# Planes made without ScalarE-GpSimd round trips, outer products first, and three images in turn

## The chip, the core and the metric

The program runs on one NeuronCore of a Trainium2 chip. Five engines work side by side, each through its own list of instructions: TensorE (PE) multiplies, VectorE (DVE), ScalarE (ACT) and GpSimd (POOL) compute, and SyncE (SP) issues most of the transfers between memory and on-chip memory; ACT and POOL issue some too. Engines wait for one another by semaphores. The metric is the device time of one execution in microseconds (us), lower is better.

## What is computed

Two layers on four images of 96 channels and 128x128 points, each layer added to its input.

```python
x = x + _L0_conv_ref(_gn(x), ...)   # projection, depthwise conv, four scans along rows/columns, norm, output projection
x = x + _L1_conv_ref(_gn(x), ...)

# layer 1, per image
xr, x1, x2 = _relu_split_norm(x, sc1, sc2, res_coef, nc1, nc2)   # two halves, each normed over the image
key, qry   = conv3x3(x1, aw1), conv3x3(x2, aw2)                  # cut into 3x3 patches
w_attn     = softmax(key . qry / sqrt(C*9))                      # 96 x 96 x 3 x 3, one per image
o          = conv3x3(conv3x3(x1, aw3), w_attn)                   # the value map, filtered by w_attn
y2         = norm(conv3x3(x2, w_conv2)) * x1
out        = xr + conv1x1([norm(o), y2], w_full)
```

`norm(o)`, the norm of x2's convolution and the split's statistics each need a whole image before the next step begins.

## The kernel before

**Stages.** The first part projects all images (L620) and scans them (L841); it ends near 3294 us. For each image the rest is: `norm` (`ssm_output`: mean and root over channels, output projection, result `xnew`; then `split_norm`: one pass over `xnew` for statistics, a second that writes the halves x1 and x2), `attend` (convolutions, attention weights, filtering) and `close` (`attn_output`: final 1x1 convolution and sum).

**Image 0** is filtered with plain maps: `direct_maps` convolves padded maps x1d and x2d (L1956) and writes the value map `vd`. **Images 1 to 3** use a product form of the 3x3 convolution: every row is cut into tiles of four columns, and six linear combinations of a tile, its planes, are multiplied by six weight matrices; four sums of the six products give the outputs. `planes_of` makes planes from a row block, `store_planes` writes them to memory (x1p, x2p, vp), `attention` loads them back in strips of 12 rows (tiles `ya`, `yc`; `yb` is a copy by ACT, L1786) and `products` multiplies. Image 0 takes this form only for its last filter, so its value map is first lifted from `vd` to planes `vp` (`lift` in `attention`, 32 blocks of four rows).

**planes_of** takes three steps of a queue `later`, one per tick: `differences` (ACT L1328 scales, POOL L1329 subtracts), `inner` (ACT L1334 and L1335 scale what L1329 wrote; POOL L1336 to L1338) and `outer` (POOL L1343 to L1345, then the store). ACT and POOL so wait for each other within one set of planes. There are 96 sets from the halves (8 rows each), 66 from value maps (`vt`, half a strip each) and 32 from `lift`.

**products and outputs.** A call makes four products (planes 1, 3, 2, 4) into two PSUM pairs `a`, `b`, then the outer two (0, 5) into a third pair `c`; three pairs exist. ACT copies `a` (L1456), DVE combines it with `b` (L1441, L1442), writes two outputs (L1445), prepares the other two (L1448, L1449) and at last adds `c` (L1466).

**Order.** `co_run(left, right, pace)` interleaves two generators while the program is written: `left` yields the cost of what it just wrote, and `right` is advanced by pace times that. Beside image b's `attend` run, in this order, `close` of image b-1 and `norm` of image b+1 at pace 0.85 (1.5 beside image 0, where only the rest of image 1's `norm` runs). After the scan the framework's planner fixes each engine's list from this order and the data's dependencies. SBUF holds two images' planes at a time in memory (`planes[b % 2]`).

**Lines touched:** L1046 `split_norm` (halves' tiles, store by ACT's queue), L1313 `planes_of`, L1358 `products`, L1425 `outputs`, L1702 `pair_sets`, L1747 `attention`, L1914 `direct_maps`, L2065 `Image`, and the driver from L2155 on.

Of the kernel before, what the change touches and what calls it, by code (L numbers as in the profile page):

```python
# [17 lines left out]
C = 96  # L18
# [18 lines left out]
AR = 12  # L37
GROUP = 9
# [29 lines left out]
def kernel(  # L68
# [101 lines left out]
    def col(name, width=1):  # L170
        return small.tile([C, width], F32, name=name, tag=name)
# [874 lines left out]
    def split_norm(xnew, x1d, x2d, stats, keep, cnt, ps, side, planes):  # L1046


        with ExitStack() as pools:
# [93 lines left out]
            shift = col("shift", 2)  # L1143
            nc.vector.tensor_mul(shift, sa, navg)
            scale = col("scale", 2)
# [8 lines left out]
            up, low = col("up", 2), col("low", 2)  # L1154
# [9 lines left out]
            thr = col("thr")  # L1164
# [4 lines left out]
            def stored(i, m, h):  # L1169
                if planes:  # L1170
                    return planes_of(
                        later, p2, h, RS, lambda pl: store_planes(nc.scalar, m, i * RS, RS, pl)
                    )
                at = (i * RS + 1) * PW
                return lambda: nc.scalar.dma_start(m[:, at : at + RS * PW], h)

            for i in range(NS):
# [3 lines left out]
                for side_, m in ((0, x1d), (1, x2d)):  # L1181
                    n = RS * PP + 4 if planes else RS * PW
                    h = p2.tile([C, n], F32, name=f"half{side_}")
# [15 lines left out]
                for _ in range(6 if planes else 1):  # L1199
                    later.tick()  # L1200
                    yield 2.0 if planes else 3.5
# [111 lines left out]
    def planes_of(later, pool, t, r, then, most=RS):  # L1313
# [3 lines left out]
        def by_k(k, n=2):  # L1317
            return t[:, k : k + r * PP].rearrange("p (t k) -> p k t", k=TW)[:, 0:n]

        a2, n = AA * AA, r * PT  # L1320
        got = []

        def differences():
            df = pool.tile([C, TW, most * PT], F32, name="df", bufs=1)[:, :, :n]
            eo = pool.tile([C, 2, most * PT], F32, name="eo", bufs=1)[:, :, :n]
            pl = pool.tile([C, NP, most * PT], F32, name="pl")[:, :, :n]
            got.extend((df, eo, pl))
            nc.scalar.mul(eo, by_k(1), a2)  # L1328
            nc.gpsimd.tensor_sub(df, by_k(2, TW), by_k(0, TW))  # L1329
            later(inner)  # L1330

        def inner():
            df, eo, pl = got
            nc.scalar.mul(pl[:, 0:NP:5], df[:, 0:2], a2)  # L1334
            nc.scalar.mul(pl[:, 3], df[:, 1], AA)  # L1335
            nc.gpsimd.tensor_sub(eo, by_k(3), eo)  # L1336
            nc.gpsimd.tensor_add(pl[:, 1], eo[:, 1], eo[:, 0])  # L1337
            nc.gpsimd.tensor_sub(pl[:, 2], eo[:, 1], eo[:, 0])  # L1338
            later(outer)

        def outer():
            df, _, pl = got
            nc.gpsimd.tensor_sub(pl[:, 0:NP:5], df[:, 2:4], pl[:, 0:NP:5])  # L1343
# [932 lines left out]
```

## Time and profile before

| | |
|---|---|
| runs | 7006.94 us median of 3 (6998.66 to 7019.27) |
| profiled execution | 6989.58 us, its span 6987.6 us |
| busy over the span | PE 5408.1 us (77%), DVE 4667.8 (67%), ACT 3838.1 (55%), POOL 3828.8 (55%) |
| mean granted PE clock | 0.858 |
| rest of `direct_maps` beside image 1's `ssm_output` | 3294 to 3590 us |
| image 0's filter beside image 1's `split_norm` | 3590 to 4050 us |
| image 1 (close 0, norm 2) | 4050 to 5065 us |
| image 2 (close 1, norm 3) | 5065 to 6085 us |
| image 3 (close 2) | 6085 to 6870 us |
| close 3 | 6870 to 6988 us |

Busy time is a share of an engine's span; an engine that is idle because another holds its input shows that as idle time before an instruction, with the releaser named. In the tables that follow, a row by stage gives the length of a stretch and the busy time of each engine in it; a group row gives count, total and mean duration of equal instructions; a wait row names the waiting engine and line, then who released it, the total, the number of times and the longest.

### The profile page before, as it was taken

To read this page: it belongs to the slowest core of one execution; us is meant where nothing else is said; L and a number is where in the kernel's file an instruction comes from. 1 tells how busy PE (TensorE), PEld (TensorE's weight loads), DVE (VectorE), ACT (ScalarE), POOL (GpSimd) and SP (SyncE) were. 2 spreads that over 40 slices of the span, in tenths; PEclk is the share of its full clock that TensorE was granted. 3 is DMA by queue.
4 is the path that set the end of the run, shared out by engine and by line. 5 is a ranking of instruction groups with operands and counts; after the bars stand their busy time and mean duration, and the time that the engine had idled before them with its cause. 6 is when DMAs were issued, how large, how long until landed. Compare 5 with 4: busy or idle time off the path is not lost.

```text
span 6987.6 us, 74482 instructions
## 1 busy us (share of the span) xinstructions
PE 5408.1 (77%) x23256; PEld 2373.8 (34%) x23256; DVE 4667.8 (67%) x6155; ACT 3838.1 (55%) x4426; POOL 3828.8 (55%) x2988
## 2 busy tenths in 40 slices
PE   5889978878886549899953368976688976688877
PEld 2323323322221114443421134444244443345542
DVE  3257879979895579897343467565776565785457
ACT  1257767777875666675354444455544464543333
POOL 2236669879794449797249942338813348723110
PEclk9999989989896669999976679987889887899888
DMA  8766777856766666756765566554675554764346
GB/s 145 179 163 179 201 205 203 233 157 197 206 171 175 175 203 196 209 170 203 190 152 146 153 161 177 160 146 122 179 190 156 158 139 129 182 185 103 89 119 172
DMA packets 886278, 1183.98 MB, mean 169 GB/s; under 512 B 208190, under 2 KB 745350, under 8 KB 873404
## 3 DMA queue, kind: packets, MB, share of 16 engines
q1 hardware_dynamic: 805436, 1065.88, 57.8%
q10 hardware_dynamic: 64240, 74.93, 3.7%
q0 software_dynamic: 16208, 38.42, 2.0%
q8 instruction: 186, 3.05, 0.2%
q14 instruction: 208, 1.70, 0.1%
HBM read 771.50 MB, written 337.56 MB: 159 GB/s over the span
## 4 chain that ended last, share of the span: by engine, by line
PE 27%; POOL 18%; issue 17%; DVE 16%; DMA 11%; ACT 9%; SPq 2%; ACTq 0%; DVEq 0%; POOLq 0%
PE bank L620 11%; PE bank L1956 5%; DVE dA L841 5%; POOL df L1329 4%; PE two L1380 3%; POOL pl L1343 3%; DVE pBC L824 2%; POOL eo L1336 2%; PE pBC L734 2%; DVE dl L845 2%; ACT yb L1786 2%; POOL pl L1345 2%; POOL pl L1338 2%; POOL pl L1337 2%; POOL pl L1344 2%
## 5 line engine op out<-in xcount | busy, mean ns | idle before, releaser
L620 PE MATMUL bank<-y,wp 128*128 128x512 f32 (+3 forms) x3584 | 1316.3, 624 | 94.4 <-DVE z L496 37.8
L853 POOL TENSOR_TENSOR y<-y,dl 128x1024 f32<-128x1024 f32 x384 | 1052.3, 2740 | 267.4 <-DVE dl L845 234.6
L820 POOL TENSOR_TENSOR dl<-dl,u 128x1024 f32<-128x1024 f32 x384 | 1008.2, 2625 | 225.9 <-ACT dA L796 111.9
L841 DVE TENSOR_TENSOR_SCAN dA<-dA,pBC 128x512 f32<-128x512 f32 x768 | 981.6, 1278 | 30.7
L620 PEld LDWEIGHTS bank<-y,wp 128*128 128x128 f32 (+3 forms) x3584 | 458.7, 169 | 764.8 <-issue 655.5
L734 PE MATMUL pBC<-xr,wbc 60*128 60x512 bf16 (+1 forms) x1536 | 456.3, 402 | 332.7 <-DVE dA L841 260.3
L1380 PE MATMUL two<-ya,wd 128*64 128x192 f32 (+3 forms) x2376 | 606.9, 437 | 136.2 <-DVE ring L1466 54.0
L845 DVE TENSOR_TENSOR dl<-dA,pBC 128x512 f32<-128x512 f32 x768 | 528.6, 688 | 267.0 <-PE pBC L734 193.6
L1956 PE MATMUL bank<-y,wn 128*128 128x384 f32 (+5 forms) x2408 | 670.4, 503 | 28.5 <-DMA y<-x1d 10.7
L1786 ACT COPY yb<-ya 64x2376 f32<-64x2376 f32 (+1 forms) x220 | 467.9, 2127 | 267.3 <-DMA ya<-x2p 105.8
L663 ACT ACTIVATE dl<-pd,dtb 128x512 f32<-128x512 f32 x768 | 486.2, 684 | 185.1 <-PE pd L734 164.7
L1380 PE MATMUL two<-yb,wd 128*64 128x192 f32 (+3 forms) x2376 | 576.2, 418 | 9.9 <-ACT yb L1786 9.9
L1380 PE MATMUL two<-ya,wa 128*96 128x384 f32 (+1 forms) x528 | 263.6, 587 | 357.5 <-DMA ya<-vp 172.4
L824 DVE TENSOR_TENSOR pBC<-dl,pBC 128x512 f32<-128x512 f32 x768 | 527.5, 687 | 8.8 <-POOL dl L820 7.9
L1441 DVE TENSOR_TENSOR sd<-sd,two 128x384 f32<-128x384 f32 (+5 forms) x176 | 137.4, 780 | 554.6 <-ACT sd L1456 541.9
L1336 POOL TENSOR_TENSOR eo<-vt,eo 96x396 f32<-96x396 f32 (+1 forms) x66 | 89.2, 1352 | 656.6 <-ACT eo L1328 656.6
L796 ACT ACTIVATE dA<-dl,negA 128x1024 f32<-128x1024 f32 x384 | 420.3, 1141 | 2.3
L1956 PEld LDWEIGHTS bank<-y,wn 128*128 128x128 f32 (+3 forms) x2408 | 306.0, 167 | 324.0 <-issue 169.0
L1380 PEld LDWEIGHTS two<-ya,wd 128*64 128x64 f32 (+1 forms) x2376 | 276.5, 177 | 396.5 <-issue 181.4
L1195 DVE SCALAR_TENSOR_TENSOR half<-xn,thr,half 96x1024 f32<-96x1024 f32 x128 | 212.9, 1675 | 259.0 <-ACT half L1190 134.5
L734 PEld LDWEIGHTS <-wbc 60*128 60x128 bf16 (+1 forms) x1536 | 103.9, 96 | 770.5 <-issue 756.7
L663 ACT ACT_TABLE_LOAD x245 | 314.3, 1283 | 93.3 <-PE pd L734 86.1
(302 smaller groups left out, 10322.7 us busy)
## 6 DMA issues: line engine op xcount, KB each, us to landing
u<-zb SPq DMA_DIRECT2D x192, 1024.0 KB
yms<-y SPq DMA_DIRECT2D x96, 512.0 KB
y<-yms SPq DMA_DIRECT2D x64, 768.0 KB
xn<-xnew SPq DMA_DIRECT2D x128, 384.0 KB
ya<-vp SPq DMA_DIRECT2D x40, 1039.5 KB
y<-y SPq DMA_DIRECT2D x128, 258.2 KB
zb<-z SPq DMA_DIRECT2D x64, 512.0 KB
ya<-x1p SPq DMA_DIRECT2D x30, 1039.5 KB
```

The source lines that it names most:

```text
L620: nc.tensor.matmul(blocks(pz[p:e]), lhsT=ws[k][:, d, c : c + e - p], rhs=window(ys[k], at, d, n), start=(i == 0), stop=(i == len(terms) - 1),)
L663: nc.scalar.activation(dst, src, AF.Softplus, bias=bias)
L734: nc.tensor.matmul(p, lhsT=w[rows], rhs=xr[rows, at : at + CH], start=True, stop=True)
L796: nc.scalar.activation(live[m]["dA"], live[m]["dl"], AF.Exp, scale=negA[:, g % 3, k : k + 1])
L820: nc.gpsimd.tensor_mul(t, t, u_view(n))
L824: nc.vector.tensor_mul(p, live[n]["dl"][:, bass.ts(half, CH)], p)
L841: nc.vector.tensor_tensor_scan(h, h, p, init, ALU.mult, ALU.add)
L845: nc.vector.tensor_mul(live[n]["dl"][:, sl], live[n]["dA"][:, sl], live[n]["C", half])
L853: nc.gpsimd.tensor_add(v, v, t.rearrange("p (a b) -> p a b", b=W))
L1380: nc.tensor.matmul(of(to[p:e], r), lhsT=w[:, i, c : c + e - p], rhs=tiles(t[k][:, i], o, r), start=(k == 0), stop=False,)
L1786: nc.scalar.copy(yb[64 * h - 64 : 64 * h, :, :n], ya[0:64, :, h * PT : h * PT + n])
L1956: nc.tensor.matmul(pc[p:e, :n].rearrange("p (h w) -> p h w", w=W), lhsT=w[:, c : c + e - p], rhs=v[:, :, 0:W], start=(i == 0), stop=(i == ...
```

## The change

**Planes.** `planes_of` no longer scales intermediate results: ACT writes two scaled copies of the input (`x4`, `x2`) in one step, and POOL makes all differences and sums from them in the next (eight instructions on the same number of elements as the seven before). A second form, `at_once`, makes the same planes on VectorE alone with seven instructions; it serves all 32 lifted blocks and, of image 1's halves, all of x2 and every second block of x1 (24 sets). The remaining 138 sets stay with ACT and POOL. Stores of the halves move from ACT's queue to SP's.

**Products.** The outer two products are made first; ACT copies them out of PSUM (`ou`), and DVE writes all four outputs after the inner four.

**Order.** Lifting moves from beside image 0's filter into `direct_maps`, up to four blocks after each set of strips, the rest at its end. `split` is cut off from `norm`. Beside image b now run the split of image b+1, the close of image b-1 and the norm of image b+2, at pace 1.0; beside image 0 the rest of image 1's split and the norm of image 2. `xnew` is kept three times, and coefficients of the split in one tile `kept`, three times. Value tile and output tile become one (`own`).

```diff
-        def differences():
-            ...
-            nc.scalar.mul(eo, by_k(1), a2)
-            nc.gpsimd.tensor_sub(df, by_k(2, TW), by_k(0, TW))
-            later(inner)
-        def inner():
-            nc.scalar.mul(pl[:, 0:NP:5], df[:, 0:2], a2)
-            nc.scalar.mul(pl[:, 3], df[:, 1], AA)
-            nc.gpsimd.tensor_sub(eo, by_k(3), eo)
-            nc.gpsimd.tensor_add(pl[:, 1], eo[:, 1], eo[:, 0])
-            nc.gpsimd.tensor_sub(pl[:, 2], eo[:, 1], eo[:, 0])
-            later(outer)
-        def outer():
-            nc.gpsimd.tensor_sub(pl[:, 0:NP:5], df[:, 2:4], pl[:, 0:NP:5])
-            nc.gpsimd.tensor_sub(pl[:, 4], df[:, 2], pl[:, 3])
-            nc.gpsimd.tensor_add(pl[:, 3], df[:, 2], pl[:, 3])
-            then(pl)
+        def at_once():
+            df, eo, pl = tile("df", TW, 1), tile("eo", 2, 1), tile("pl", NP, bufs)
+            stt = nc.vector.scalar_tensor_tensor
+            nc.vector.tensor_sub(df, by_k(t, 2, TW), by_k(t, 0, TW))
+            stt(eo, by_k(t, 1), -a2, by_k(t, 3), ALU.mult, ALU.add)
+            nc.vector.tensor_add(pl[:, 1], eo[:, 1], eo[:, 0])
+            nc.vector.tensor_sub(pl[:, 2], eo[:, 1], eo[:, 0])
+            stt(pl[:, 0:NP:5], df[:, 0:2], -a2, df[:, 2:4], ALU.mult, ALU.add)
+            for i, f in ((3, AA), (4, -AA)):
+                stt(pl[:, i], df[:, 1], f, df[:, 2], ALU.mult, ALU.add)
+            later(lambda: then(pl))
+        def scaled():
+            x4 = pool.tile([C, most * PP], F32, name="x4", bufs=1)[:, : r * PP]
+            x2 = tile("x2", 2, 1)
+            nc.scalar.mul(x4, t[:, : r * PP], a2)
+            nc.scalar.mul(x2, by_k(t, 1, TW)[:, 0:TW:2], AA)
+            later(lambda: differences(x4, x2))
+        def differences(x4, x2):
+            f, pl = tile("df", TW, 1), tile("pl", NP, bufs)
+            nc.gpsimd.tensor_sub(f, by_k(t, 2, TW), by_k(x4, 0, TW))
+            nc.gpsimd.tensor_sub(x2[:, 0], x2[:, 1], x2[:, 0])
+            nc.gpsimd.tensor_sub(x2[:, 1], by_k(t, 4)[:, 0], by_k(t, 2)[:, 0])
+            nc.gpsimd.tensor_sub(pl[:, 0:NP:5], f[:, 2:4], f[:, 0:2])
+            for i, x in ((1, f[:, 1:3]), (3, x2)):
+                nc.gpsimd.tensor_add(pl[:, i], x[:, 1], x[:, 0])
+                nc.gpsimd.tensor_sub(pl[:, i + 1], x[:, 1], x[:, 0])
+            later(lambda: then(pl), 2)
+        return at_once if vector else scaled
...
     # split_norm: store of a half's planes
-                        later, p2, h, RS, lambda pl: store_planes(nc.scalar, m, i * RS, RS, pl)
+                        later, p2, h, RS, lambda pl: store_planes(nc.sync, m, i * RS, RS, pl),
+                        vector=vector(i, m is x2d),
...
-                    yield 2.0 if planes else 3.5
+                    yield 2.5 if planes else 3.5
...
     # products: the two outer products are made ahead of the four
+        outer, sums = evac
+        ...
+        outer(a)
         a, b = pairs_of(ps), pairs_of(ps)
         ...
-        finish(c)
...
     # outputs
+                nc.scalar.copy(got[1], c[:m, :, :n])
...
+                nc.vector.tensor_add(u, u, got[0][:, :, 0])
+                    for k, x, f, y in (
+                        (0, s[p:e, 1], 1.0, u[p:e, 0]),
+                        (1, d[p:e, 1], AA, d[p:e, 0]),
+                        (2, s[p:e, 1], AA * AA, s[p:e, 0]),
+                        (3, d[p:e, 1], AA * AA * AA, u[p:e, 1]),
+                    ):
...
     # direct_maps
+            def lift(rows):
+                for _ in range(4 if rows < H else H // LR):
+                    ...
+                    nc.sync.dma_start(to, src[:, :, 1:PW])
+                    later(planes_of(
+                        later, img.lifts, h, LR, lambda pl, a=a: store_planes(nc.sync, img.vp, a, LR, pl),
+                        LR, True,
+                    ), 2)
+                    yield 1.2
+            yield from pair_sets(img, taps, later, p2, 3, inputs, convolve, lift)
+            yield from lift(H)
...
     # driver
+    light = chain(
+        imgs[1].norm(yms[0][1], psr, "right"),
+        imgs[1].split(psr, "right", lambda i, second: second or i % 2 > 0),
+    )
...
+        if 0 < b and b + 1 < NB:
+            after.append(imgs[b + 1].split(psr, "right"))
         if b:
-            light.append(imgs[b - 1].close(psr, "right"))
-        if b + 1 == 1:
-            light.append(next_norm)
-        elif b + 1 < NB:
-            imgs[b + 1] = Image(b + 1)
-            light.append(imgs[b + 1].norm(yms[(b + 1) // 2][(b + 1) % 2], psr, "right"))
+            after.append(imgs[b - 1].close(psr, "right"))
+        if b + 2 < NB:
+            imgs[b + 2] = Image(b + 2)
+            after.append(imgs[b + 2].norm(yms[b // 2 + 1][b % 2], psr, "right"))
-        co_run(left, light, 0.85 if b else 1.5)
+        co_run(left, light, 1.0 if b else 1.5)
         drain(left)
         drain(light)
```

## The prediction

> **What bounds the kernel now.** I read the table by stage first, since the average over the span mixes a scan, convolutions and small tails. All instruction lists are equal up to the end of the scan (3294 us); only what follows counts. Columns: length, then busy us of PE, weight loads, DVE, ACT, POOL, then clock, DMA share, GB/s.
>
> ```profile
> 3294.00:3590.00 296.00, 268.64 (x1125) 121.01 (x1121) 108.92 (x222) 124.77 (x196) 59.93 (x65) 0.95 0.65 175
> 3590.00:4050.00 460.00, 142.86 (x408) 60.72 (x408) 177.67 (x195) 199.64 (x264) 417.16 (x629) 0.62 0.60 152
> 4860.00:5065.00 205.00, 132.80 (x405) 57.76 (x405) 151.00 (x147) 108.95 (x105) 171.43 (x176) 0.79 0.64 165
> 6310.00:6720.00 410.00, 336.67 (x2338) 225.56 (x2336) 203.48 (x320) 165.89 (x161) 94.06 (x112) 0.87 0.40 97
> 6720.00:6870.00 150.00, 117.68 (x412) 52.99 (x412) 89.03 (x129) 50.35 (x33) 0.00 (x0) 0.88 0.55 140
> ```
>
> Row 1 is PE bound (91%). In row 2 POOL is busy 91% and PE 31%: image 0's filter waits for planes. Rows 4 and 5 are image 3 with nothing beside it: PE is 82% busy in the strips. The statistics L1868 of its strips start 51.1 us apart (6311 to 6669); beside `ssm_output` of image 3, in image 2, they are 78.6 us apart (5291 to 5606, four strips), beside `close` 63 to 79.
>
> Next the waits, for 3590 to 4050 (first four) and 6360 to 6710 (last two):
>
> ```profile
> PE two L1380 <- DMA ya<-vp: 172.4, 8, 42.6
> ACT pl L1334 <- POOL df L1329: 117.1, 45, 8.1
> ACT eo L1328 <- POOL pl L1338: 56.9, 26, 5.3
> SPq L1352 <- POOL pl L1345: 209.7, 30, 15.2
> PE two L1645 <- ACT sd L1456: 41.7, 14, 4.8
> ACT pl L1334 <- POOL df L1329: 36.1, 14, 3.9
> ```
>
> PE waits for `vp`, which SP stores only when POOL has made it. Even alone, image 3's transposes wait 41.7 us in some seven strips for ACT's copy, and in the same stretch ACT stands 36.1 us behind a scaling that waits for POOL.
>
> The groups give the price of planes (3590 to 4050: first two; 4683 to 5036: third and fourth; 6310 to 6720: last):
>
> ```profile
> L1329 POOL TENSOR_TENSOR df<-half 96x1056 f32<-96x1056 f32 x30 | 66.6, 2219 | 22.0 <-DVE half L1195 20.7
> L1329 POOL TENSOR_TENSOR df<-lift 96x528 f32<-96x528 f32 x32 | 38.8, 1212 | 5.1 <-DMA lift<-vd 4.9
> L1448 DVE TENSOR_TENSOR sd<-sd 96x384 f32<-96x384 f32 x8 | 11.2, 1399 | 0.0
> L1195 DVE SCALAR_TENSOR_TENSOR half<-xn,thr,half 96x1024 f32<-96x1024 f32 x30 | 48.9, 1637 | 32.5 <-ACT half L1190 17.2 <-POOL eo L1336 15.1
> L1448 DVE TENSOR_TENSOR sd<-sd 128x384 f32<-128x384 f32 x14 | 8.4, 599 | 0.0
> ```
>
> [...] L1448 takes 599 ns where POOL is 23% busy and 1399 ns where it makes planes. [...]
>
> **The change part by part.**
>
> *Planes on POOL.* Summed over its seven rows a half's set takes 9.1 us, a lift's 5.0 us. The new eight have the same elements; I take the same. 24 halves and 32 lifts leave POOL: 24 x 9.1 + 32 x 5.0 = 378 us, nearly all from 3590 to 4050.
>
> *Planes on DVE.* No row shows them. [...] I take 3.05 and 5.0: 32 x 3.05 + 24 x 5.0 = 218 us.
>
> *ACT.* Per half before 1156 + 642 + 411 ns; after, two scalings of 1056 and 528 elements, about 1.17 + 1.16. Copying the outer products adds 0.79 or 0.48 us a call, 118 us over all images; the removed sets give 81, and fewer intermediate scalings some more. ACT is at most 45% busy, so this is free. What counts is the wait: it now depends on POOL only through single buffers `x4`, `x2`. This frees part of the 41.7 us above: 15 us per image for images 1 to 3, -45 (bounds 0 and -41.7 x 11/7 x 3 = -197).
>
> *Outputs.* DVE per 128-row call: before 2 x 0.954 + 2 x 0.912 + 0.599 + 0.567 + 1.553 = 6.45 us, after 2 x 0.954 + 0.957 + 4 x 0.912 = 6.51. Nothing in time, but elements with two SBUF inputs rise from 1536 to 2304. The outer pair comes free by an ACT copy while the four products run, so PE need not wait for it; covered by these, at worst 0.8 us a call.
>
> *Lifting in `direct_maps`.* In the built order 20 lifts stand before the softmax, 12 between it and the last product weight. The 20 cost DVE 61 us of 187 idle ones, but their loads and stores stand in SP's list ahead of loads `y<-x1d` of a PE-bound stretch: 0 to 60 us, I take 10. The 12, with three sets of a half, six halves and the weights themselves, are 37 + 16 + 9 + 4 = 66 us of DVE ahead of `watd`, which took 9 us from L1593 to its issue: +57. Without this cover the same work would lie in row 2.
>
> *Image 0's filter with image 1's split.* DVE has left: 20 sets x 5.0 + 26 halves x 1.3 + 11 strips x 8.4 (two at 0.95, one at 0.96, four at 0.88, three statistics at 0.68) = 226 us; at 87% filling 260. POOL has 8 sets, 73 us. So DVE replaces POOL as bound.
>
> *Norm of image 2.* The split uses up the pace; in the built order all of this norm's PE work follows the filter's last product, and SP's first `y<-yms` stands behind the split's last store. It runs alone. Its round is a chain (copy L960, transfer `mq<-st`, DVE, root, ACT, PE): copies L960 start 14.1 us apart beside `direct_maps`, 18.2 beside image 1, and 7.6 at the shortest. Alone I take 10: 16 x 10 + 20 = 180 us (142 to 246).
>
> So image 1 starts at 3590 + 10 + 57 + 260 + 180, and 10 for statistics and first loads: 4107. Before, its first product is at 4080. **+30**.
>
> *Image 1.* Same content as before (split, close, norm), other order: 0. The bounds: ACT freed earlier, -60; POOL and DVE exclude each other more beside strips, +60.
>
> *Image 2.* Loses a norm: 4 x (78.6 - 51.1) = **-110**. Image 3 keeps its content. Stores from ACT's to SP's list: 96 x 0.5 us of issuing leave ACT; on SP they wait for POOL with `ya` loads behind them, which are issued half a strip ahead (25 us) of their use; that hides a POOL up to that late. Beyond, PE waits for each.
>
> Sum: 30 + 0 - 110 - 45 = -125 by the middles. The unpriced risks (SP's order, exclusion) are one-sided, so I give back 25: **-100**. Span 6987.6 - 100 = 6888; the profiled execution would be 6890, and since the median lies 17 above the profiled run, 6905 us.
>
> **Rivals.**
> - *More is freed.* ACT no longer holds PE, 100 of the 197, and the norm's round takes 8: 6905 - 55 - 30 = 6820. For: min round 7.6. Against: `x2` is one buffer that POOL frees with its last two instructions.
> - *The lone norm eats it.* Round 14.1 as beside `direct_maps` (+66) and DVE sets at 5.6 (+15), SP costs 20: 7005, no change. For: the chain is mostly latency. Against: beside `direct_maps` it waits for a PE that is 97% busy (235.9 of 244).
> - *Slower: exclusion beside strips.* Split now goes beside 6.2 strips of 38.6 cost units (240 / 38.6) in images 1 and 2. Per strip POOL has 5.2 halves' sets and two `vt` sets: 5.2 x 9.1 + 2 x 7.1 = 62 us, DVE 8 us of new and 6 of old two-input work. If none overlaps, a strip takes 76 instead of about 65, and with ACT held by `x2` 82: 2 x 6.2 x 17 = +210: 7115. It decides against me when such strips pass 73 us. For: L1448's 1399. Against: POOL's 9.1 already has such waiting in it.
> - *The change doesn't do what it says:* ACT still waits as long for POOL. Then only -110 + 30 is left, inside the main range.
>
> **Numbers.** Main 0.50 (6845 to 6980), more 0.15, lone norm 0.13, exclusion 0.22. A difference under 0.3% (21 us) can't be told from none. Faster: 0.49 + 0.15 = 0.64; same 0.14; slower 0.22. The range from 6800 to 7060 leaves out half of each outer case.
>
> **What would show it.** Right: no `ACT pl` wait on POOL; image 1's first product near 4110; copies L960 of image 2 about 10 us apart with PE near idle; image 2 near 910 us instead of 1015. Wrong: a lone norm over 240 us, PE waiting for `y<-x1d` before 3590, strips beside the split over 73 us, or SP waits for POOL that end in PE waits for `ya`.

## The result, and the profile after

The changed kernel takes **7238.23 us** (median of 4 runs, 7229.39 to 7246.84) against 7006.11 us of the kernel before in the same group of runs: ratio **1.033**, 95% interval 1.0309 to 1.0349. It is slower by 232 us, where 100 us less were forecast. The profiled execution took 7246.84 us, its span is 7245.1 us. All times by stage below are taken from the profiled executions; medians of different groups of runs are compared through their ratio to the kernel before, which ran beside each group.

I cut the part after the scan into stages: image b runs from its first product to the first product of image b+1; image 3 ends with the statistics of its last output rows.

| us | before | after | difference |
|---|---|---|---|
| image 0's first filter product at | 3637 | 3740 | +103 |
| image 0 (filter, and after it the lone norm) | 391 | 533 | +142 |
| image 1 | 1050 | 1108 | +58 |
| image 2 | 1018 | 1010 | -8 |
| image 3 | 770 | 725 | -45 |
| close 3 | 122 | 128 | +6 |

Table by stage of the kernel after. Columns: length, busy us of PE, weight loads, DVE, ACT, POOL, then clock, DMA share, GB/s:

```profile
3640.00:3740.00 100.00, 5.01 (x21) 2.99 (x19) 89.21 (x183) 25.89 (x23) 34.17 (x76) 0.52 0.62 150
3740.00:3940.00 200.00, 130.69 (x396) 54.55 (x396) 161.95 (x190) 83.15 (x64) 60.72 (x74) 0.78 0.67 170
3940.00:4030.00 90.00, 3.19 (x10) 0.55 (x10) 65.78 (x81) 15.38 (x14) 27.25 (x45) 0.51 0.46 127
4030.00:4260.00 230.00, 164.16 (x375) 37.23 (x374) 71.49 (x127) 64.14 (x79) 56.04 (x64) 0.63 0.49 133
4345.00:4810.00 465.00, 263.36 (x1610) 163.85 (x1610) 275.90 (x272) 224.55 (x212) 416.01 (x407) 0.76 0.39 101
6580.00:6960.00 380.00, 326.04 (x2314) 213.43 (x2312) 191.31 (x319) 178.81 (x173) 120.61 (x133) 0.90 0.41 99
```

Row 1: TensorE stands for 100 us before the first filter product. Row 2: the filter itself is short: from its first product to the statistics of its last outputs it takes 209 us, before 379. Rows 3 and 4: 90 us nearly without TensorE, then the norm of image 2 alone. Row 5 is the split of image 2 beside image 1's strips: **POOL is busy 416 of 465 us (89%)** and PE 57%. The strips' statistics there are some 82 us apart (from 4334 to 4827); 73 us was the point at which the prediction called itself wrong. From the first to the last masking of its halves (the VectorE instruction that writes a half, L1195 before and L1201 after) this split takes 460 us; before it took 356. Row 6 is image 3 in its strips. The row of before for its split of image 2, in the same columns:

```profile
4683.00:5036.00 353.00, 230.45 (x1064) 128.40 (x1061) 230.87 (x246) 189.76 (x203) 307.63 (x331) 0.76 0.56 145
```

The granted clock does not explain the longer split: it is 0.76 there before and after.

The groups on POOL tell why. First the kernel before in that stretch (not shown in the prediction), then after in 4345 to 4810; busy us and mean ns stand behind the bar:

```profile
L1329 POOL TENSOR_TENSOR df<-half 96x1056 f32<-96x1056 f32 x30 | 68.4, 2281 | 3.6 <-DVE half L1195 1.4
L1336 POOL TENSOR_TENSOR eo<-half,eo 96x528 f32<-96x528 f32 x30 | 51.6, 1719 | 33.6 <-ACT eo L1328 33.6
```

```profile
L1352 POOL TENSOR_TENSOR df<-half,x 96x1056 f32<-96x1056 f32 x29 | 124.6, 4296 | 13.3 <-ACT x L1346 13.3
L1355 POOL TENSOR_TENSOR pl<-df 96x528 f32<-96x528 f32 x29 | 43.2, 1490 | 5.8 <-DMA x2p<-pl 3.6 <-DMA x1p<-pl 2.1
L1352 POOL TENSOR_TENSOR df<-own,x 96x792 f32<-96x792 f32 x12 | 39.1, 3255 | 0.0
```

The first instruction of a set has the same 1056 elements as before and takes **4296 instead of 2281 ns**. The other rows hardly differ. Summed over its eight rows a half's set takes 11.35 us; before, in its stretch, seven rows sum to 9.28. Before subtracts two views of one tile, two elements apart; after subtracts the view of `half` from a view of the scaled copy `x4`, another tile, both with a step of four elements.

How POOL's time reaches TensorE is in the waits, 4345 to 4810:

```profile
ACT x L1346 <- POOL df L1352: 80.9, 25, 8.0
ACT x L1347 <- POOL pl L1358: 78.7, 19, 9.4
ACT half L1196 <- POOL x L1354: 40.3, 21, 6.2
PE two L1393 <- ACT sd L1480: 77.7, 10, 15.1
PE two L1655 <- ACT ou L1456: 43.4, 8, 13.7
PE two L1655 <- ACT sd L1480: 29.8, 8, 12.8
```

In the kernel before the same waits, 4683 to 5036, were:

```profile
ACT eo L1328 <- POOL pl L1338: 43.0, 13, 7.5
ACT pl L1334 <- POOL df L1329: 41.1, 20, 8.0
ACT eo L1328 <- POOL pl L1345: 18.6, 4, 5.7
PE two L1380 <- ACT sd L1456: 22.3, 7, 8.1
PE two L1645 <- ACT sd L1456: 16.2, 5, 8.7
PE two L1541 <- ACT sd L1456: 11.1, 2, 10.0
```

After, ACT stands 200 of 465 us behind POOL, for the single `x4` and `x2` and for a free `half`; before, these rows sum to 103 of 353 us. In ACT's list its copies `sd` and `ou` out of PSUM stand behind such waits, and PE waits 151 us for them in the rows of after, 50 in those of before. The round trips within a set are gone as the change says; a wait for a free buffer has taken their place.

### The profile page after: what moved, and what is told of

Read it like the earlier page. It is cut to its first block, busy times and chain, and to the rows that moved or that the text cites. A ratio compares the mean times of both kernels' runs of the same rounds, so it can differ in the third digit from the quotient of the medians.

```text
span 7245.1 us, 74140 instructions
## 1 busy us (share of the span) xinstructions
PE 5487.0 (76%) x23256; PEld 2382.5 (33%) x23256; DVE 4907.5 (68%) x6580; ACT 3876.0 (53%) x4296; POOL 3731.4 (52%) x2734
## 3 DMA queue, kind: packets, MB, share of 16 engines
q8 instruction: 186, 3.05, 0.2%
## 5 line engine op out<-in xcount | busy, mean ns | idle before, releaser
L1393 PE MATMUL two<-ya,wd 128*64 128x192 f32 (+3 forms) x2376 | 622.3, 446 | 330.7 <-ACT sd L1480 219.1
L1393 PE MATMUL two<-yb,wd 128*64 128x192 f32 (+3 forms) x2376 | 594.2, 427 | 3.7 <-ACT yb L1797 3.7
L1464 DVE TENSOR_TENSOR sd<-sd,two 128x384 f32<-128x384 f32 (+5 forms) x176 | 137.6, 782 | 586.9 <-ACT sd L1480 577.9
L1352 POOL TENSOR_TENSOR df<-own,x 96x792 f32<-96x792 f32 (+1 forms) x66 | 208.6, 3161 | 372.9 <-ACT x L1346 372.2
L949 PE MATMUL bank<-y,mean 96*32 96x512 f32 x512 | 256.3, 793 | 168.7 <-DMA y<-yms 101.7
L1393 PEld LDWEIGHTS two<-yb,wd 128*64 128x64 f32 (+1 forms) x2376 | 311.4, 180 | 170.9 <-issue 51.2
L1201 DVE SCALAR_TENSOR_TENSOR half<-xn,kept,half 96x1024 f32<-96x1024 f32 x128 | 215.4, 1697 | 210.5 <-ACT half L1196 177.2
```

The source lines that it names most:

```text
L1393: nc.tensor.matmul(of(to[p:e], r), lhsT=w[:, i, c : c + e - p], rhs=tiles(t[k][:, i], o, r), start=(k == 0), stop=False,)
```

## The experiments

Ratios are to the kernel before. The stages are of the profiled executions, in the order of the table above.

| run | ratio (95% interval) | first filter product | image 0, 1, 2, 3, close 3 |
|---|---|---|---|
| after | 1.0329 (1.0309 to 1.0349) | 3740 | 533, 1108, 1010, 725, 128 |
| E2 old planes in the new order | 1.0093 (1.0076 to 1.0111) | 3748 | 524, 1044, 929, 701, 124 |
| E3 `x4` packed | 1.0215 (1.0197 to 1.0234) | 3736 | 519, 1066, 972, 722, 128 |
| E4 before + new planes | 1.0391 (1.0372 to 1.0409) | 3650 | 454, 1168, 1103, 785, 125 |
| E5 before + new products | 0.9893 (0.9866 to 0.9920) | 3621 | 381, 1035, 1006, 733, 128 |
| E6 after, `df` packed | 1.0000 (0.9987 to 1.0013) | 3712 | 512, 1013, 919, 693, 124 |
| E7 E6 in the old order | 0.9956 (0.9946 to 0.9966) | 3721 | 279, 1057, 1050, 736, 126 |
| E8 E7, lifts on POOL | 1.0003 (0.9992 to 1.0013) | 3749 | 277, 1045, 1045, 721, 120 |
| E9 E5 + packed planes | 0.9827 (0.9811 to 0.9844) | 3640 | 358, 1023, 983, 732, 128 |
| E10 E9, `x4` in place, two buffers | 0.9846 (0.9831 to 0.9861) | 3643 | 354, 1047, 993, 720, 125 |
| E11 E10, x2 of image 1 on DVE | 0.9795 (0.9778 to 0.9811) | 3637 | 377, 989, 996, 723, 120 |
| E12 E7, lifts beside the filter | 1.0085 (1.0070 to 1.0100) | 3646 | 371, 1134, 1059, 733, 122 |
| E13 E8, lifts on POOL's queue | 1.0004 (0.9991 to 1.0016) | 3753 | 285, 1059, 1058, 733, 128 |
| E14 E7, old pace, stores on ACT | **0.9740** (0.9713 to 0.9767) | 3754 | 247, 966, 984, 740, 125 |
| E15 E7, stores on ACT | 0.9827 (0.9801 to 0.9854) | 3749 | 247, 1037, 1007, 710, 123 |
| E16 E6, stores on ACT | 0.9963 (0.9951 to 0.9975) | 3740 | 475, 1003, 919, 706, 128 |

**My theory** after the result: the layout of POOL's first instruction costs the time. **Rivals:** POOL waits for VectorE (exclusion, which the prediction had named); the new order (lone norm, crowded split) costs it whatever the planes cost; ACT is held by its single buffers.

### E1: POOL's subtraction by layout, alone

```python
for _ in range(8):                       # a, b: tiles; by4: a view with a step of four; to4: packed
    sub(to4(o["near2"]), by4(a, 2), by4(a, 0))
    sub(to4(o["near8"]), by4(a, 8), by4(a, 0))
    sub(to4(o["near16"]), by4(a, 16), by4(a, 0))
    ...
    sub(to4(o["b2"]), by4(a, 2), by4(b, 0))
    sub(to4(o["bpack"]), by4(a, 2), to4(b))
    sub(o["packpack"], flat(a, 0), flat(b, 0))
    sub(by4(o["wide"], 0), to4(a[:, 2:]), to4(b))    # packed reads, strided write
```

> Only GpSimd's subtraction of 96 x 1056 fp32 elements in 16 layouts, a subtraction of 528 in two, and one copy, eight times each, with VectorE idle; the rest of the program is left out and the output is zeros. Theory (layout): the first instruction of a set takes 4.2 us after and 2.1 us before because of where its two inputs lie: two inputs with a step of four elements take about 2.1 us when they are the same tile two elements apart (near2), about 4.2 us when they lie in two tiles (b2, b0); one strided and one packed input takes about 3.1 us (bpack, packa), as 1575 ns for 528 does before; two packed about 2.6 (packpack). If the distance counts and not the tile, near8 to near256 climb to 4.2 and far, in the same tile, has it too. Rival (exclusion): the 4.2 us are waiting for VectorE; then all strided forms take about 2.1 us here.

Groups of the run (columns as above); L96 is near2, L97 near8, L98 near16, L103 b2, L105 bpack, L107 packpack, L110 wide; L108 is packed inputs in one tile, two elements apart, and L113 a copy read at a step of four:

```profile
L98 POOL TENSOR_TENSOR o_near<-a 96x1056 f32<-96x1056 f32 x8 | 33.2, 4147 | 0.0
L103 POOL TENSOR_TENSOR o_b<-a,b 96x1056 f32<-96x1056 f32 x8 | 33.1, 4138 | 0.0
L97 POOL TENSOR_TENSOR o_near<-a 96x1056 f32<-96x1056 f32 x8 | 23.8, 2971 | 0.0
L105 POOL TENSOR_TENSOR o_bpack<-a,b 96x1056 f32<-96x1056 f32 x8 | 23.4, 2925 | 0.0
L107 POOL TENSOR_TENSOR o_packpack<-a,b 96x1056 f32<-96x1056 f32 x8 | 19.2, 2404 | 0.0
L110 POOL TENSOR_TENSOR o_wide<-a,b 96x1056 f32<-96x1056 f32 x8 | 16.5, 2058 | 0.0
L96 POOL TENSOR_TENSOR o_near<-a 96x1056 f32<-96x1056 f32 x8 | 16.4, 2044 | 14.6 <-DVE o_near L77 14.5
L108 POOL TENSOR_TENSOR o_packnear<-a 96x1056 f32<-96x1056 f32 x8 | 15.5, 1942 | 0.0
L113 POOL COPY o_gather<-a 96x1056 f32<-96x1056 f32 x8 | 16.3, 2036 | 0.0
```

With VectorE idle the instruction takes 4138 ns for two strided inputs in two tiles and 2044 for two views two elements apart: the factor of two is the layout, and **exclusion is refuted as the cause of this instruction's time**. It is the distance, not the tile: eight elements apart in one tile it takes 2971, sixteen and more 4147. One strided and one packed input take 2925, two packed 1942 to 2404 by where they lie, and the form with a strided write (2058) lies within these. Against packed inputs from the same two tiles (2404 and 2058 ns), a single strided input adds 22 to 42% (2925) and two far apart add 72 to 101% (4138). Why eight elements apart (2971) lies between is not shown.

### E2, E3, E6: three ways to take the strided pair away

E2 makes POOL's sets in the old way:

```diff
-        return at_once if vector else scaled
+        return at_once if vector else differences   # the old differences, inner, outer
```

> After, but the 138 sets of planes that GpSimd makes are made in the old way (ScalarE scales intermediate results, three steps), in the new order, with the new products and with VectorE's 56 sets. Theory (layout): GpSimd's set is back at 9.1 us, the two split stages fall from 464 to about 390 us, image 1 from 1105 to about 1010 and image 2 from 1006 to about 930: 7060 us. Rival (order: the lone norm and a split beside six strips instead of eight cost the time, whatever form the planes have): 7200 us or more, since ScalarE also waits for GpSimd again.

E3 lets ACT write `x4` packed, so one input stays strided:

```diff
-            x4 = pool.tile([C, most * PP], F32, name="x4", bufs=1)[:, : r * PP]
+            x4 = tile("x4", TW, 1)
...
-            nc.scalar.mul(x4, t[:, : r * PP], a2)
+            nc.scalar.mul(x4, by_k(t, 0, TW), a2)
...
-            nc.gpsimd.tensor_sub(f, by_k(t, 2, TW), by_k(x4, 0, TW))
+            nc.gpsimd.tensor_sub(f, by_k(t, 2, TW), x4)
```

> After, but ScalarE writes the scaled copy x4 by planes (packed), so that GpSimd's first instruction reads one strided and one packed input instead of two strided ones. Theory (layout): that instruction takes about 3.1 instead of 4.2 us, 138 times 0.75 to 1.1 us = 125 us off GpSimd in all, the split stages 464 to about 430 us, images 1 and 2 some 35 us shorter each, image 3 and image 0 little: 7160 us. Rival (order): 7225 us or more.

E6 reads and writes in row order; the later instructions then read `f` at a step of four, one or two elements apart:

```diff
-            f, pl = tile("df", TW, 1), tile("pl", NP, bufs)
-            nc.gpsimd.tensor_sub(f, by_k(t, 2, TW), by_k(x4, 0, TW))
+            f, pl = pool.tile([C, most * PP], F32, name="df", bufs=1), tile("pl", NP, bufs)
+            nc.gpsimd.tensor_sub(f[:, : r * PP], t[:, 2 : 2 + r * PP], x4)
+            f = by_k(f, 0, TW)
```

> After, but GpSimd's first instruction of a set reads its two inputs packed (row order) and writes its result packed; the later ones read that result two elements apart in one tile. Theory (layout): the first instruction takes about 2.1 us instead of 4.2, a half's set about 7.6 us instead of 11.2 (9.1 before), the split stages about 370 us, image 1 about 1020, image 2 about 910: 7030 us, a little under the run with the old planes, as ScalarE no longer waits within a set. Rival (ScalarE held through the single buffers x4 and x2 counts, not GpSimd's durations): little over half of the gain, 7120 us or more.

The first instruction in the split of image 2, in E2, E3 and E6 in this order:

```profile
L1351 POOL TENSOR_TENSOR df<-half 96x1056 f32<-96x1056 f32 x32 | 71.6, 2236 | 14.2 <-DVE half L1201 13.4
```

```profile
L1352 POOL TENSOR_TENSOR df<-half,x 96x1056 f32<-96x1056 f32 x32 | 99.5, 3110 | 16.0 <-ACT x L1346 16.0
```

```profile
L1352 POOL TENSOR_TENSOR df<-half,x 96x1056 f32<-96x1056 f32 x32 | 72.4, 2264 | 14.6 <-ACT x L1346 14.6
```

It takes 2236, 3110 and 2264 ns, and the kernels take 7072, 7154 and 6993 us where 7060, 7160 and 7030 were expected. From the first to the last masking of its halves, the split of image 2 takes 460 us after, 429 in E3, 411 in E2 and 386 in E6. With E6's three lines the ratio goes from 1.0329 to 1.0000, and in the split (4300 to 4690) ACT's waits for POOL fall from 200 to 125 us and PE's for `sd` and `ou` from 151 to 104. The loss follows the duration of this instruction, but not alone: E2 and E6 have it equal and differ by 65 us. A half's set sums to 9.07 us in E2 and to 8.71 in E6 (7.6 were expected), and E2 has the old waits of ACT within a set; how the 65 us divide between the two is not shown. Of the 104 us by which the split grew, E6 gives back 74. In the rest of it POOL has 12 sets of value maps to make where five stood before, since the new order puts the split beside other strips.

VectorE pays too. Its instruction L1474 (L1475 in E6), both inputs in one tile, in the split after (4345 to 4810) and then in E6 (4300 to 4690):

```profile
L1474 DVE SCALAR_TENSOR_TENSOR ring<-sd 128x384 f32<-128x384 f32 x22 | 41.2, 1872 | 0.0
L1475 DVE SCALAR_TENSOR_TENSOR ring<-sd 128x384 f32<-128x384 f32 x22 | 28.5, 1296 | 0.0
```

It takes 1872 ns on average beside the long instruction of POOL and 1296 beside the short one. The timeline of after has a single case: POOL's L1352 starts at 4516.35 and takes 4.19 us; the L1474 that starts at 4518.36 takes 2.90 us and ends 0.7 us after it; the next one of the same shape, at 4521.95 with POOL idle, takes 0.91. The other direction is in the timeline of before: POOL's L1338 (264 elements), started at 4786.30, 0.06 us after VectorE's L1195 (1.28 us), takes 1.82 us, and at 4804.51, with VectorE idle, 0.74. VectorE's L1464, with one input in PSUM (128x768), takes 951 ns in the split after and 954 in image 3's strips (6580 to 6960). This is what the prediction calls exclusion. It didn't make POOL's instruction long (E1), but it may pass that length on to VectorE; no run tests this by itself.

The rival that ACT's single buffers hold the gain back (7120 or more) is refuted by E6, which keeps them. The rival order is refuted as the main cause: E2 and E3 keep the order and stay below the 7200 and 7225 us that it asked for. But E2 is still 0.9% slower than before, and E6 no faster; what the rest of the change costs is what the next runs are about.

### E4 and E5: one part of the change alone

E4 is before with the new form on POOL for all sets (and three buffers of halves). E5 is before with the new `products` and `outputs` (and one tile for values and outputs).

> Before, with only the new form of planes on ScalarE and GpSimd for all 194 sets (none on VectorE), old order, old products; the halves share three buffers instead of four, for space. Theory (layout): the filter of image 0, where GpSimd is 91% busy, gets longer by 32 x 1.1 + 24 x 2.2 = about 85 us, the split stages beside images 1 and 2 by about 60 us each, the value maps' sets are hidden: about 7210 us. Rival (order): 7006 within 30 us, or faster as ScalarE no longer waits for GpSimd within a set.

> Before, with only the new products and outputs (outer two products first, four outputs after the inner four, value and output tile in one for space); planes and order are old. Theory (the new products free TensorE, as image 3 got 70 us shorter in the runs with new products): image 3 about 715 instead of 770 us, images 1 and 2 about 20 us shorter each, as GpSimd's pace beside them hides some: 6910 us. Rival (the new products cost nothing and bring nothing, image 3 got shorter by the new planes of its value map): 7000 within 15 us.

E4 takes 7279 us, 70 more than expected, and loses where that was expected: image 0's filter +63 us (+85 expected), images 1 and 2 +118 and +85 (+60 each expected). So the new form of the planes loses without any of the new order. That its layout does this, and not its single buffers, is told by E9 below: there the same form with packed inputs, put on E5, gains.

E5 takes 6910 us, as expected: the new products alone save 75 us (56 to 94 by the interval), 37 of them in image 3 (55 were expected there). PE's waits for ACT's copies in image 3, before (6096 to 6866) and then E5 (6044 to 6777):

```profile
PE two L1645 <- ACT sd L1456: 48.2, 16, 5.7
PE two L1380 <- ACT sd L1456: 10.4, 4, 3.3
```

```profile
PE two L1380 <- ACT sd L1467: 22.0, 9, 3.8
PE two L1642 <- ACT sd L1467: 7.1, 8, 1.7
PE two L1642 <- ACT ou L1443: 5.4, 3, 2.8
```

They fall from 59 to 35 us, with PE's busy time nearly equal (639 and 643 us): 24 of the 37 us. So the change holds one part that gains and one that loses.

### E7, E12: the order

E7 is E6 with the old order beside images 1 and 2 (VectorE's sets and the lifting in the convolutions stay):

```diff
-        if 0 < b and b + 1 < NB:
-            after.append(imgs[b + 1].split(psr, "right"))
...
-        if b + 2 < NB:
-            imgs[b + 2] = Image(b + 2)
-            after.append(imgs[b + 2].norm(yms[b // 2 + 1][b % 2], psr, "right"))
+        if 0 < b and b + 1 < NB:
+            imgs[b + 1] = Image(b + 1)
+            after.append(imgs[b + 1].norm(yms[(b + 1) // 2][(b + 1) % 2], psr, "right"))
+            after.append(imgs[b + 1].split(psr, "right"))
```

> As the run before, and the order beside images 1 and 2 is the old one (close b-1, norm b+1, split b+1), so that nothing but the rest of image 1's split stands beside image 0's filter and no norm runs alone; VectorE's planes, the lifting in the convolutions and the new products stay. Theory (second cause: the lone norm costs 220 us and 90 us of waiting for its first input, and image 2 got only 89 us shorter by it): image 1's first product comes near 3960, image 2 gets about 90 us longer: 6830 us. Rival (the time only moves: images 1 and 2 get longer by what image 0 loses): 7000 us or more.

The lone norm goes, image 0 is 233 us shorter, and image 1's first product comes at 4000 (3960 expected). But images 1 and 2 become 44 and 131 us longer and image 3 43: the medians fall only from 6993 to 6954 us, not to 6830. **The expectation was wrong**; the new order is no great loss in itself. It costs 233 us at image 0 and gets nearly all of it back in images 1 to 3; by the medians 39 us are missing.

E12 puts the lifting of E7 back beside image 0's filter, on ACT and POOL (the function `lift` is left out here):

```diff
-    imgs[0].lifts = lifting.enter_context(tc.tile_pool(name="lifts", bufs=2, side="right"))
...
+            for i in range(3):
+                lift(i)              # in attention, and lift(i + 3) after each strip, as before
```

> As the run with the old order, packed df and VectorE's halves, but the lifting stands beside image 0's filter again, on ScalarE and GpSimd. Theory (in the convolutions the lifts hold SP: their loads and stores wait for buffers with the convolutions' loads and the filter's first load behind them, so the first filter product comes at 3721 to 3749 instead of 3637): first filter product again near 3635, filter about 290 us, 50 us under the run with the old order. Rival (it only moves work: the filter gets longer by as much as its start comes earlier): within 15 us of it.

The first filter product comes at 3646 as expected, but the part of image 0 takes 371 us instead of 279 and image 1 1134 instead of 1057; the time is 7064 us, by the ratios 90 us more than E7, where 50 less were expected. The first 250 us of image 1, in E12 and then in E7 (columns as in the tables by stage):

```profile
4017.00:4267.00 250.00, 175.94 (x779) 87.62 (x779) 221.31 (x265) 100.31 (x90) 74.31 (x84) 0.79 0.64 171
```

```profile
4000.00:4250.00 250.00, 219.90 (x983) 103.98 (x984) 176.66 (x220) 112.98 (x105) 53.96 (x52) 0.84 0.66 175
```

DVE is busy 221 us there instead of 177, PE 176 instead of 220. The last masking of image 1's own split lies at 4088 in E12, after the filter's end, and at 3975 in E7: without the 38 cost units that lifting yields in the convolutions (32 blocks of 1.2), less of that split is written beside them, and it spills into image 1. So E12 changes two things at once, the place of the lifts and how far the split gets; that the second is all of the 77 us in image 1 is argued, not shown.

### E8, E13: why image 0's filter starts late

E8 makes E7's lifts on ACT and POOL (`LR, True` becomes `LR`); E13 also issues their loads and stores from POOL's queue instead of SP's.

> As the run before, and the 32 lifted blocks are made by ScalarE and GpSimd instead of VectorE, in the same place. Theory (VectorE's lifts stand ahead of the softmax and the product weights and delay image 0's first filter product from 3637 to 3740): the first filter product comes 40 us earlier, 6795 us. Rival (what comes late there is the convolutions' own work behind the lifts' transfers on SP, not VectorE): within 10 us of the run before.

> As the run with the lifts on GpSimd in the convolutions, but the lifts' loads and stores are issued from GpSimd's queue instead of SP's. Theory (SP, held by the lifts' waits for buffers, issues the filter's first load late): PE's wait for the first load of the value map (77 us there) shrinks to 20 us or less, the first filter product comes near 3680 instead of 3749, and the time falls by about 60 us against that run. Rival (the data are late: softmax, product weights and the last lifted block itself end near 3720 whatever queue): the wait only changes its name, within 20 us of that run.

Both theories fall. The first filter product comes at 3721 in E7, 3749 in E8, 3753 in E13. What it waits for, in E8 and then E13 (3290 to 3800; who waits, for whom, total us, times, longest):

```profile
PE two L1394 <- DMA yc<-vp: 77.2, 1, 77.2
PE bank L1613 <- DVE sm L1605: 25.9, 1, 25.9
```

```profile
PE two L1394 <- DMA wa<-watd: 51.1, 2, 45.7
PE bank L949 <- ACT sq L942: 40.3, 11, 7.4
```

With VectorE free of lifts, the values are still late; with SP free of them, the product weights are, and ACT's square holds the norm beside the convolutions for 40 us. The wait only changes its name, as E13's rival had it. Neither VectorE's work nor SP's queue is alone the cause; what else delays this stretch when lifts stand in it stays open.

### E9, E10, E11: the good parts on the kernel before

E9 is E5 with E6's packed planes (and, for space, three buffers of halves and one of the value map's planes). E10 writes the first result over `x4`, with two buffers of `x4` and `x2` in the split. E11 lets VectorE make image 1's 16 sets of x2.

```diff
-            x4 = pool.tile([C, most * PP], F32, name="x4", bufs=1)[:, : r * PP]
-            x2 = tile("x2", 2, 1)
+            x4 = pool.tile([C, most * PP], F32, name="x4", bufs=2)[:, : r * PP]     # E10
+            x2 = tile("x2", 2, 2 if most == RS else 1)
...
-            nc.gpsimd.tensor_sub(f[:, : r * PP], t[:, 2 : 2 + r * PP], x4)
+            nc.gpsimd.tensor_sub(x4, t[:, 2 : 2 + r * PP], x4)
...
+                        vector=vector and m is x2d,                                 # E11, vector: b == 1
```

> Before, with the new products, and with planes in the new form on ScalarE and GpSimd for all 194 sets, the first instruction packed as in the run with packed df; old order, lifting beside image 0's filter, ScalarE's stores, nothing on VectorE (three buffers for the halves, one for the value map's planes, for space). Theory (a set is 7.6 instead of 9.1 us): image 0's filter, which waits for GpSimd's planes, takes about 325 instead of 381 us; images 1 to 3 stay: 6860 us. Rival (ScalarE is held by the single x4 and x2 as long as it was by GpSimd within a set, so images 1 and 2 lose what image 0 gains): 6910 us or more, the time with the new products alone.

> As the run before, but GpSimd writes its first result over x4, and x4 and x2 have two buffers in the split, so that ScalarE can scale a set while GpSimd is at the one before. Theory (ScalarE's waits for x4 and x2, 108 us an image, hold its copies out of PSUM and so TensorE): 20 to 40 us less in each of images 1 and 2: 50 us under the run before. Rival (GpSimd's and TensorE's own pace set these stages; ScalarE has slack): within 10 us of it.

> As the run before, and VectorE makes the 16 sets of image 1's second half (x2). Theory (GpSimd bounds image 0's filter and VectorE has room there): some 13 sets of 7.6 us leave GpSimd there, image 0's filter gets 40 us shorter, all else stays. Rival (VectorE's sets of 6.4 us and its exclusion with GpSimd take it back): within 10 us.

E9: 6879 us against 6860 expected and 6910 of E5; image 0 gains 23, not 56. A half's set there sums to 8.4 us and not to the 7.6 that the expectation took (8.8 before), which makes the gain small. E10: 6894, no gain, its interval overlaps E9's; so in the old order, with the cheaper planes, ACT's wait for `x4` and `x2` costs nothing that two buffers give back. E11: 6860, 34 less than E10, but not where expected: image 0 takes 377, not less than the 354 of E10, and image 1 is 58 us shorter. That vector sets help is shown; by what path is not.

### E14, E15, E16: the stores' queue and the pace

E7 and E9 make equally cheap planes, yet images 1 and 2 take 1057 and 1050 us in E7 and 1023 and 983 in E9. E14 gives E7 the old pace, with the old cost units of the split, and the old queue; E15 only the queue; E16 gives E6 (the new order) the queue.

```diff
-                        later, p2, h, RS, lambda pl: store_planes(nc.sync, m, i * RS, RS, pl),
+                        later, p2, h, RS, lambda pl: store_planes(nc.scalar, m, i * RS, RS, pl),   # E14, E15, E16
...
-                    yield 2.5 if planes else 3.5
+                    yield 2.0 if planes else 3.5                                                  # E14 only
...
-        co_run(left, light, 1.0 if b else 1.5)
+        co_run(left, light, 0.85 if b else 1.5)                                                   # E14 only
```

> As the run with the old order and packed df, with the old cost units of the split (2.0), the old pace (0.85) and the halves' stores on ScalarE's queue again. Images 1 and 2 took 1057 and 1050 us in that run, and 1023 and 983 in the run with the same planes made from before's side. Theory (SP's queue and the crowded split cost this): 6890 us, 60 us under the run with the old order. Rival (the difference lies elsewhere, as in the buffers of lifts and halves, or in the granted clock): 6940 us or more.

> As the run with the old order and packed df, with one edit: the halves' planes are stored from ScalarE's queue instead of SP's; cost units 2.5 and pace 1.0 stay. Theory (SP's queue: a store that waits for GpSimd holds the strips' loads behind it, which the run with old pace and old queue cured): ratio to before about 0.978, 6850 us. Rival (the pace did it: the split of the next image is spread and crowded differently): within 0.004 of the run with the old order (ratio 0.9956).

> As the run after with packed df (new order, lone norm), with one edit: the halves' planes are stored from ScalarE's queue. Theory (SP's queue): images 1 and 2 some 30 to 40 us shorter each, ratio about 0.99. Rival (pace; or in this order SP's wait is hidden): ratio 0.998 or more.

E14 takes 6824 us, more gain than expected and the fastest of all: ratio 0.974, against 1.033 of the changed kernel. E15 (0.9827) tells that the queue gives 0.013 (90 us) of it and the pace with the cost units 0.009 (61 us). In the new order the queue gives only 0.0037 (26 us, E16: 0.9963, between the 0.99 expected by the theory and the 0.998 of its rival). Waits over images 1 and 2 in E7, then E15:

```profile
PE two L1394 <- ACT sd L1481: 152.8, 22, 15.6
SPq L1366 <- POOL pl L1359: 347.9, 51, 20.9
ACT x L1347 <- POOL pl L1359: 214.8, 57, 11.0
```

```profile
PE two L1394 <- ACT sd L1481: 92.7, 16, 15.7
SPq L1366 <- POOL pl L1359: 260.0, 34, 18.1
ACT x L1347 <- POOL pl L1359: 134.0, 43, 6.9
```

With the halves' stores on SP it stands 348 us behind POOL, and PE 153 us behind ACT's copy. With the stores on ACT these are 260 and 93, and even ACT waits less for POOL (134 instead of 215), although it now issues stores that wait for POOL. The path from SP's stand to ACT's copies (late loads of strips, `yb` copied late, the copies out of PSUM behind it) is argued; the times are shown.

## Why the prediction was wrong

The forecast was 6905 us, in a range from 6800 to 7060; 7238 were measured. By its steps:

**Planes on POOL: this step failed.** "The new eight have the same elements; I take the same" put a half's set at 9.1 us. It takes 11.35, because elements were counted and not where they lie. E1 measures the layout alone, E2, E3 and E6 take it away in three ways or in part, E4 adds the new form alone. In the new order it costs 0.033 of the time, about 230 us, against the packed form (E6), and 0.024, about 165 us, against the old form (E2). The profile before had a hint that I didn't read: L1336, one strided and one packed input, takes 1719 ns for 528 elements (3.3 ns each) while L1329, two strided views two elements apart, takes 2281 for 1056 (2.2 each). The price of an element on POOL already differed by half with the layout, and the new first instruction had a third layout, which no row showed. It was an operation to be bounded from both sides, and I gave it no bound.

**The rival "exclusion beside strips" had the place and the strips' time** (82 us, with POOL full and ACT held by `x2`), but less than half of the loss (7115 us), and another mechanism: POOL's instruction takes its 4.1 us with VectorE idle. That its 82 us came out is luck. It was right that the order puts the split beside six strips, so that a fuller POOL lands on TensorE.

**Scaling on ACT.** "No ACT `pl` wait on POOL" came true, and "it now depends on POOL only through single buffers" became 160 us of waiting for `x4` and `x2` in one split. With the cheaper planes and the old order this is not what holds it (E10). "At most 45% busy" was misread as well: the prediction's own row from 4860 to 5065 has ACT at 53%. The -45 that this term was given is not measured by itself. The nearest is E9 against E5, where ACT's waits within a set go and POOL's work gets a little cheaper: 36 us in images 1 to 3.

**Image 1's first product** was forecast at 4107 and came at 4273. By terms: the filter starts at 3740 instead of 3657 (+83; the 10 for SP's loads and the 57 for VectorE's work were too small, and E8 and E13 show that neither engine alone explains it); the filter takes 209 instead of 260 us (-51), although VectorE's sets cost 3.3 and 6.45 us instead of the 3.05 and 5.0 of my estimate, which no row of the profile showed; then the norm's PE work begins 78 us after the statistics of the filter's last outputs, for want of its first input. That was seen ("SP's first load stands behind the split's last store") and given no price. The waits of PE after, 3590 to 4270, the first ahead of the filter, the second ahead of the norm:

```profile
PE two L1393 <- DMA yc<-vp: 91.3, 1, 91.3
PE bank L949 <- DMA y<-yms: 89.8, 1, 89.8
```

The lone norm's PE work takes 227 instead of 180 us (+47): its copies are 13.8 us apart, not 10, near the 14.1 of the rival "the lone norm eats it". What follows it takes 19 instead of 10 us (+9). The terms sum to the 166 us that are missing. The prediction's 4080 for the kernel before is also wrong: its first product lies at 4028.5. With that the same terms give +79 instead of +30, and the whole forecast shrinks from -100 to about -50.

**Image 2, -110**, was nearly right once the layout is taken away: in E6 image 2 takes 919 against 1018 (-99), of which 12 are due to the new products (E5), and image 1 1013 against 1050. The layout had eaten it. Image 3, which was to keep its content, is 43 us shorter in the new order than in the old (693 in E6, 736 in E7); why stays open.

**New products, "nothing in time"**: -75 measured (E5). The prediction asked only whether the outer pair would cost anything, and gave no price to PE's wait for ACT's copies that it takes away.

**Stores from ACT to SP**, priced at nothing as long as POOL is less than 25 us late: 26 us in the new order (E16), 90 in the old (E15). So the waits were not covered.

So layout is the cause of the sign, but without it the change would have made no difference (E6, 1.0000), not -100: image 1 starts 196 us later, by the late filter, the wait for the norm's first input and the lone norm, and images 1 to 3 give back 213.

## What to carry to other kernels

Price an instruction by the row that has its layout, not only its size: steps, distance between inputs, packed or not; where no row has it, give it bounds and measure it by itself first. In the split POOL was nearly full (87% busy before, 89% after); 2.07 us more for a half's set (11.35 against 9.28) went with a split 104 us longer, of which E6 gives 74 back. So price the work of a helper engine that is nearly full with most care. A change of several parts can hide a gain of one (products 75 us) and a loss of another behind one sum. E14 has the new products, the planes with packed inputs, VectorE's sets and the lifting in the convolutions, and the order, the pace and the stores' queue of the kernel before.

## What the runs showed of the hardware

All for GpSimd's fp32 subtraction of 96 x 1056, VectorE idle: 1942 to 2404 ns with both inputs packed; 2044 with both at a step of four elements, two elements apart; 2971 at eight elements; 4138 to 4147 at sixteen and beyond, in one tile or two; 2925 with one packed; 2058 with packed inputs and a write at a step of four. A copy read at a step of four takes 2036.
